# A graph kernel's first pairs: scores spread on chip, roots per graph, constants moved behind the first propagation

## The chip, the cores and the metric

The kernel runs on one core of a Trainium2 chip. The metric is the device time of one execution in microseconds (us); several executions are made and their median is given. All engines of the core run side by side, each taking its own instructions in the order in which they were written: TensorE (PE; its weight loads are PEld), VectorE (DVE), ScalarE (ACT), GpSimd (POOL), and SyncE (SP), which here only issues DMAs. ACT issues some DMAs too.

## The reference

There are 128 graphs of 128 nodes with 512 features (x) and a 0/1 adjacency matrix each (adj). Two layers are applied, each followed by a residual and a normalization over the features. Layer 0 is graph attention with 8 heads of 64 units, layer 1 a hypergraph convolution used twice.

```
# layer 0
feats   = einsum('bnf,hfu->bhnu', X, W)
dense   = e_self[..., :, None] + e_neigh[..., None, :]     # feats . a_self, feats . a_neigh
dense   = leaky_relu(dense, 0.2) + NEG_BIG * (1 - A)
out     = relu(softmax(dense) @ feats + b)                 # heads side by side: 512 features
x       = layernorm(x + out)
# layer 1
conv(x, W) = Dn * (H @ (Be * (H^T @ (x @ W^T)))) + b       # H = (adj != 0)
h       = layer_norm(relu(conv(x, W1) + b1), gamma, beta)  # 1024 features
x       = layernorm(x + conv(h, W2) + x)
```

Everything is float32.

## The kernel before, in words

The work is cut into 64 pairs of graphs. Nothing is a loop at run time: a Python list `todo` of (due time, function, arguments) is sorted by due time and walked once, and each function writes its instructions to the engines. Only the order counts; the due times are sort keys (period T = 38.6), not times on the chip. Steps of a pair are spread over about five periods (`lag`), so that several pairs are in work at once. A dictionary `first` overrides the key of single steps of the first pairs, and a second list places steps that only pairs 0 and 1 have.

For one pair, the stages are as follows.

- Loads: x, adjacency (a), its first row spread over the partitions (w), and block-wise copies (xb, ab) for pairs from 2 on, whose transposes are made by DVE (L385, L421). Pairs 0 and 1 have their transposes made by PE (L397, L410).
- Nodes and edges: `nodes` (L360 to L369) and `edges` (L423 to L428) make the two degree factors, `scale_edges` (L435) scales, `propagator` forms the product pd on PE, and `r_evict` (L451) makes R from it and from the node factors dnb, which go through DRAM to be spread.
- Features: x times the attention weights w0 (pf). Each head has two extra weight columns, so that the self and neighbour scores come out beside the features. Pairs from 2 on use a seven-product scheme on sums of blocks; pairs 0 and 1 use plain products (L523) and copies (L533).
- Scores: the neighbour scores are transposed by DVE (`rows`, L542), written to DRAM (rd, L550 or L552) and read back spread over all partitions (nb, L570). POOL adds the mask (L589), ACT applies the leaky step with the self score as bias (L605), DVE takes the largest (nm, L611), ACT the exponential (L619), each for a quarter (graph g, half q of the heads) at a time.
- Attention: the exponentials are transposed (eT; for pair 0 by PE, L651, and copied, L652), multiplied with the features and a column of ones (pav, L677 or L703), divided (rden, y; L713, L714), joined with x (L751), and normalized: moments (L759, L760), ve (L765), the root on POOL (rs, L767), and the normalization on ACT (L785 to L794).
- Propagation and layer 1: pz = y times R on PE, copied to zT by ACT (`z_evict`, L829), block differences zS on POOL (L840), the hidden layer in seven products phX, phY, phW, which DVE sums (h, L866) and ACT finishes (relu L881, square L892), its squares summed by POOL (L904), then the output layer (py), the second propagation (pq), and the last normalization and store.

The prologue also makes constants. The score columns of w0 are made by products of the raw weights with the attention vectors, DVE doing the self and POOL the neighbour vector (`prepare_first`, L234, L238), from vectors that two DMAs spread over the partitions. Seven-product sums of w0 (`prepare_first_sums`, L226), of w1 (`prepare_hidden`, L249) and of w2 follow. gamma and beta are folded into w2: column sums of w2 on PE (pv, L276, `prepare_output`), spread by two products gw and bw (L288), and each block of w2 scaled and shifted by DVE (L300, 16 instructions).

[...] PE's pieces of 64 columns (`columns`, L97) are written in pairs to two halves of a bank.

Of the kernel before, what the change touches and what calls it, by code (L numbers as in the profile page):

```python
# [8 lines left out]
F32 = mybir.dt.float32  # L9
AF = mybir.ActivationFunctionType  # L10
# [3 lines left out]
EPS = 1e-5  # L14
# [6 lines left out]
def kernel(  # L21
# [143 lines left out]
    def everywhere(t, ap, queue):  # L165
        queue.dma_start(t, ap.partition_broadcast(P))

    as_bc, an_bc = (
        work.tile([P, F], F32, tag="eb", name=n, bufs=2) for n in ("as_bc", "an_bc")
    )  # L170
# [6 lines left out]
    everywhere(an_bc, a_neigh, nc.scalar)  # L177
    everywhere(as_bc, a_self, nc.scalar)
# [6 lines left out]
    vec_rows = work.tile([3 * KH, P], F32, tag="neg", name="vec_rows", bufs=2)  # L185
    for i, ap in enumerate((gamma, beta, b1)):
        nc.sync.dma_start(vec_rows[i * KH:(i + 1) * KH], ap.rearrange("(k p) -> k p", p=P))
# [20 lines left out]
    nc.gpsimd.memset(mhalf, -0.5)  # L208

    fts = []  # L210
# [16 lines left out]

    def prepare_first(half):
        for n, (dst, raw, j) in list(enumerate(w0_blocks))[2 * half:2 * half + 2]:
            nc.scalar.copy(dst[:, :, :, 2:], raw)  # L230
            for c, bc in enumerate((as_bc, an_bc)):
                t = work.tile([P, KF // 2, HH, U], F32, tag=(("o", "xS"), ("o", "zS"))[n % 2][c],
                              name=f"wa{n}{c}", bufs=(2, 1)[c])
                (nc.vector, nc.gpsimd)[c].tensor_tensor(  # L234
                    t, raw, bc[:, j * QU:(j + 1) * QU].rearrange("p (h u) -> p h u", h=HH)
                    [:, None].to_broadcast([P, KF // 2, HH, U]), op=ALU.mult,
                )
                nc.vector.tensor_reduce(dst[:, :, :, c], t, AX.X, ALU.add)  # L238

    def prepare_first_sums():  # L240
        second_sums(nc.vector, [w0_sb[:, i] for i in range(7)], w0_12)
# [9 lines left out]
    gbs = const.tile([P, KH, 2], F32, name="gbs")  # L251
    made = {}
# [12 lines left out]
    def prepare_rows():  # L265

        made["sel"] = work.tile([2, 2, P], F32, tag="zT", name="sel")
        nc.gpsimd.tensor_copy(
            made["sel"], ident[:2, :2].unsqueeze(2).to_broadcast([2, 2, P])
        )  # L270

    def prepare_output():
        pv = made["pv"] = [bank(f"pv{j}") for j in range(2)]
        for blk, i, j in w2_blocks:
            for k in range(KH // 2):
                nc.tensor.matmul(  # L276
                    pv[j][:2, :QU], gbs[:, i * KH // 2 + k, :], blk[:, k, :],
                    start=(i == 0 and k == 0), stop=(i == 1 and k == KH // 2 - 1),
                )

    def prepare_output_sums():
        made["sums"] = const.tile([2, F], F32, name="sums")
        for j in range(2):
            nc.vector.tensor_copy(made["sums"][:, j * QU:(j + 1) * QU], made["pv"][j][:2, :QU])
# [108 lines left out]
    def x_transpose_first(p, s):  # L393
        s["px"] = [bank(f"px_{p}_{g}") for g in range(2)]
        for g in range(2):
            for k in range(KF):
                nc.tensor.transpose(  # L397
                    s["px"][g][:, k * N:(k + 1) * N],
                    s["x"][:, g].rearrange("p (f k) -> p k f", k=KF)[:, k], ident,
                )  # L400

    def x_transpose_out(p, s, g):
        if g == 0:
            s["xT"] = work.tile([P, 2, KF, N], F32, tag="xT", name=f"xT_{p}")
        nc.scalar.copy(s["xT"][:, g].rearrange("p k n -> p (k n)"), s["px"][g])
# [110 lines left out]
    def plain_features(p, s, i):  # L516
        if i == 0:
            s["pf"] = [[bank(f"pf_{p}_{g}{j}") for j in range(2)] for g in range(2)]
        for j in range(2):
            w = (w0_sb[:, 0], w0_12, w0_sb[:, 1], w0_sb[:, 2])[2 * i + j]  # L520
            for g in range(2):
                for k in range(KF // 2):
                    nc.tensor.matmul(  # L523
                        s["pf"][g][j][:, :FW], s["xT"][:, g, i * KF // 2 + k, :],
# [4 lines left out]
    def plain_features_out(p, s):  # L529
        s["ft"] = fts[p]  # L530
        for j in range(2):
            for g in range(2):
                (nc.vector.tensor_copy if g or p else nc.scalar.copy)(  # L533
                    s["ft"][:, g, j * HH:(j + 1) * HH, :UW], by_head(s["pf"][g][j])
                )

    @step(1, 25.0)
    def spread_rows(p, s):
# [7 lines left out]
        shape = [B, NB, B] if p == 0 else [NB, B, B]  # L546
        rd = s["rd"] = dram.tile(shape, F32, tag="rd", name=f"rd_{p}")
        if p == 0:
            for b in range(NB):
                (nc.sync, nc.scalar)[b % 2].dma_start(rd[:, b, :], rows[b * B:(b + 1) * B])  # L550
        else:
            nc.sync.dma_start(rd.rearrange("b c j -> (b c) j"), rows)  # L552

    def blocked(p, t):

        dims = "p (h b j) -> p b h j" if p == 0 else "p (b h j) -> p b h j"
        return t.rearrange(dims, b=NB, h=H)

    @step(1, 27.0)
    def neighbours(p, s):  # L560
        s["nb"] = work.tile([P, 2, H * N], F32, tag="nb", name=f"nb_{p}")
        for g in range(2):
            dst, src, hs = s["nb"][:, g, :], s["rd"], slice((2 + g) * H, (3 + g) * H)
            if p == 0:
                src = src[hs].rearrange("h b j -> (h b j)")
            else:
                dst = dst.rearrange("p (b x) -> p b x", b=NB)
                src = src[:, hs, :].rearrange("b h j -> b (h j)")
            queue = nc.scalar if p == 0 and g == 1 else nc.sync
            queue.dma_start(dst, src.partition_broadcast(P))  # L570
# [10 lines left out]
    def scores(p, s, g, hs):  # L581
        return blocked(p, s["nb"][:, g, :])[:, :, hs, :]
# [10 lines left out]
    def leaky(p, s, g, q):  # L593
        if (p, g, q) == (0, 1, 1):

            hs = slice(HH, H)
            t = s["nb"][:, g, HH * N:].rearrange("p (h j) -> p h j", h=HH)
            nc.vector.tensor_tensor(
                t, t, s["ft"][:, g, hs, 0:1].to_broadcast([P, HH, N]), op=ALU.add
            )  # L600
            nc.vector.scalar_tensor_tensor(t, t, SLOPE, t, op0=ALU.mult, op1=ALU.max)
            return
# [33 lines left out]
    def e_transpose(p, s, g, q):  # L636
# [6 lines left out]
        )  # L643

    def e_transpose_first(p, s, g, q):
        if (g, q) == (0, 0):
            s["eT"] = work.tile([P, 2, H, N], F32, tag="eT", name=f"eT_{p}")
        t = bank(f"pet_{g}{q}")
        for h in range(HH):
            n = (q * HH + h) * N  # L650
            nc.tensor.transpose(t[:, h * N:(h + 1) * N], s["nb"][:, g, n:n + N], ident)  # L651
        (nc.scalar.copy if q else nc.vector.tensor_copy)(  # L652
            s["eT"][:, g, q * HH:(q + 1) * HH, :].rearrange("p h n -> p (h n)"), t
        )
# [52 lines left out]
    def attended(p, s, g):  # L707
        if g == 0:
            s["y"] = work.tile([P, 2, F], F32, tag="y", name=f"y_{p}")
        rden = small.tile([P, 2, HH], F32, tag="rden", name=f"rden_{p}_{g}")  # L710
        for q in range(2):
# [410 lines left out]
    for t, fn, *args in (  # L1122
# [14 lines left out]
    T = 38.6  # L1137
    todo = [
        (11.1, prepare_first, (0,)), (12.0, prepare_first, (1,)), (15.45, prepare_first_sums, ()),
        (12.1, load_weights, (nc.scalar, w2_blocks, w2t, DH // 2, QU)),  # L1140
        (13.05, prepare_vectors, ()),
        (14.05, load_weights, (nc.scalar, w1_blocks[:2], w1t, F // 2, HALF)),
        (12.95, load_first_row, (1,)),
        (15.46, load_weights, (nc.sync, w1_blocks[:1:-1], w1t, F // 2, HALF)),
        (16.1, everywhere, (b2_bc, b2, nc.sync)),
        (79.0, prepare_hidden, (nc.gpsimd, 0)), (79.1, prepare_hidden, (nc.gpsimd, 1)),
        (120.7, prepare_hidden, (nc.gpsimd, 2)), (110.6, prepare_hidden, (nc.vector, 3)),
        (15.5, prepare_output_vectors, ()), (16.0, prepare_output, ()),
        (78.3, prepare_rows, ()), (78.79, prepare_output_sums, ()),
        (78.99, prepare_output_spread, (0, "gw")), (98.0, prepare_output_spread, (1, "bw")),  # L1150
        (98.1, prepare_output_bias, ()), (98.2, prepare_output_blocks, (slice(0, 1),)),
        (99.75, prepare_output_blocks, (slice(1, 2),)),
        (117.8, prepare_output_blocks, (slice(2, 3),)),
        (118.1, prepare_output_blocks, (slice(3, 4),)),
# [7 lines left out]
        ("spread_rows", 0): 13.5, ("neighbours", 0): 14.0,  # L1162
        ("nodes", 0): 12.9, ("write_nodes", 0): 12.92, ("spread_nodes", 0): 15.9,
        ("edges", 0): 14.46, ("edges", 2): 119.2,
        ("x_transpose", 2, 0): 120.5, ("x_transpose", 2, 1): 121.1, ("scale_edges", 0): 14.47, ("propagator", 0): 14.55,
        ("r_evict", 0): 97.845,
        ("spread_rows", 1): 15.72, ("nodes", 1): 15.55, ("write_nodes", 1): 15.85,
        ("edges", 1): 110.4, ("scale_edges", 1): 110.5, ("neighbours", 1): 80.1,
        ("propagator", 1): 121.7, ("spread_nodes", 1): 80.3, ("r_evict", 1): 121.8,
        ("leaky", 0, 1, 1): 77.65, ("leaky", 0, 0, 1): 73.6, ("largest", 0, 0, 1): 75.3,  # L1170
# [105 lines left out]
```

## Time and profile before

| what | value |
|---|---|
| median of 3 executions | 2398.43 us (2396.28 to 2400.03) |
| the profiled execution itself | 2395.3 us |
| its span, first to last instruction | 2393.4 us |
| busy in the span | PE 2360.8, DVE 2089.6, POOL 1825.6, ACT 1528.5 |
| busy from 0 to 47.2 us (first pz) | PE 34.28, DVE 32.09, POOL 22.13, ACT 18.23 |
| busy from 47.2 to 87.06 us (second pz) | PE 37.88, DVE 39.13, POOL 34.69, ACT 24.09 |

A line of a timeline gives the start, the duration, the engine, the line of the kernel, the operation, the tile written and the tiles read, and the number of instructions merged in it (x32); in brackets stands how long the engine had been idle before it and what it waited for. The chain of waits is the list of work that ended last, followed back from the end: at each moment it names the one piece that everything later depended on. Busy time is no bound by itself: an engine that is idle nearly everywhere can still hold the one instruction that the others wait for.

### The profile page before, as it was taken

To read this page: it belongs to the slowest core of one execution; us is meant where nothing else is said; L and a number is where in the kernel's file an instruction comes from. 1 tells how busy PE (TensorE), PEld (TensorE's weight loads), DVE (VectorE), ACT (ScalarE), POOL (GpSimd) and SP (SyncE) were. 2 spreads that over 40 slices of the span, in tenths; PEclk is the share of its full clock that TensorE was granted. 3 is DMA by queue.
4 is the path that set the end of the run, shared out by engine and by line. 5 is a ranking of instruction groups with operands and counts; after the bars stand their busy time and mean duration, and the time that the engine had idled before them with its cause. 6 is when DMAs were issued, how large, how long until landed. Compare 5 with 4: busy or idle time off the path is not lost.

```text
span 2393.4 us, 80729 instructions
## 1 busy us (share of the span) xinstructions
PE 2360.8 (99%) x32309; PEld 2026.8 (85%) x32309; DVE 2089.6 (87%) x4456; ACT 1528.5 (64%) x4481; POOL 1825.6 (76%) x2060
## 2 busy tenths in 40 slices
PE   7899999999999999999999999999999999999998
PEld 6788887888888888888888888888888888888886
DVE  7989888898898898898898888988988988988975
ACT  4565765756667667667667666666676676676662
POOL 5877786777877877877877778778778778778774
PEclk9999999999999999999999999999999999999999
DMA  6555454555554555555545555544545555555541
GB/s 197 133 148 150 143 144 134 159 143 147 151 148 144 149 148 148 151 143 154 144 142 157 141 147 155 146 146 147 150 143 153 147 150 139 148 156 140 149 128 37
DMA packets 431134, 347.09 MB, mean 145 GB/s; under 512 B 151440, under 2 KB 380328, under 8 KB 430760
## 3 DMA queue, kind: packets, MB, share of 16 engines
q1 hardware_dynamic: 427288, 337.46, 49.5%
q8 instruction: 256, 4.19, 0.7%
q10 hardware_dynamic: 3472, 4.47, 0.6%
q14 instruction: 118, 0.97, 0.2%
HBM read 239.08 MB, written 102.73 MB: 143 GB/s over the span
## 4 chain that ended last, share of the span: by engine, by line
PE 89%; DMA 4%; DVE 3%; ACT 1%; POOL 1%; issue 1%; SPq 1%; DVEq 0%; POOLq 0%; ACTq 0%
PE phX L97 17%; PE pyX L97 17%; PE pfX L97 8%; PE pyW L97 8%; PE phW L97 8%; PE pav L703 5%; PE phY L97 4%; PE pz L97 4%; PE pfW L97 4%; PE pq L97 4%; PE pyY L97 4%; PE pfY L97 2%; DMA ed<-nb 1%; PE pd L97 1%; DMA nb<-rd 1%
## 5 line engine op out<-in xcount | busy, mean ns | idle before, releaser
L344 ACT COPY py<-pyX 128x257 f32<-128x257 f32 x189 | 70.7, 374 | 538.5 <-PE pyX L97 465.6
L97 PEld LDWEIGHTS phX<-zS,w_sb 128*64 128x64 f32 x6144 | 350.6, 137 | 36.3 <-POOL ft L742 23.1
L97 PE MATMUL phX<-zS,w_sb 128*64 128x128 f32 x6144 | 373.4, 273 | 2.6 <-ACT ph L344 2.6
L904 POOL TENSOR_TENSOR sq<-sq 128x512 f32<-128x512 f32 (+2 forms) x384 | 343.9, 896 | 20.1
L589 POOL TENSOR_TENSOR nb<-nb,neg 128x512 f32<-128x512 f32 x256 | 319.9, 1284 | 23.1 <-DMA nb<-rd 12.7
L605 ACT ACTIVATE nb<-nb,ft 128x128 f32<-128x128 f32 x1020 | 325.1, 392 | 13.7 <-POOL nb L589 13.7
L619 ACT ACTIVATE nb<-nb,nm 128x128 f32<-128x128 f32 x1024 | 319.4, 392 | 4.2 <-DVE nm L611 4.0
L767 POOL TENSOR_TENSOR rso<-veo,mhalf 128x2 f32<-128x2 f32 x63 | 44.2, 701 | 338.4 <-DVE veo L765 338.4
L97 PE MATMUL pyX<-w_sb,hS 128*64 128x257 f32 x2016 | 245.1, 380 | 0.0
L97 PE MATMUL pyX<-w_sb,h 128*64 128x257 f32 x2016 | 243.7, 379 | 0.5 <-ACT py L344 0.5
L97 PE MATMUL pyW<-w_sb,hS 128*64 128x256 f32 x2016 | 243.3, 378 | 0.0
L881 ACT ACTIVATE h<-h,vecs 128x128 f32<-128x128 f32 x768 | 239.4, 394 | 2.0 <-DVE h L866 1.4
L611 DVE TENSOR_REDUCE nm<-nb 128x4 f32<-128x512 f32 x256 | 175.2, 684 | 48.8 <-ACT nb L605 46.2
L97 PEld LDWEIGHTS pyX<-w_sb,h 128*64 128x64 f32 x2016 | 173.7, 136 | 46.2 <-ACT py L344 0.9
L97 PEld LDWEIGHTS pyW<-w_sb,hS 128*64 128x64 f32 x2016 | 174.7, 136 | 43.6 <-issue 0.3
L742 POOL TENSOR_TENSOR ft<-ft,b_bc 128x512 f32<-128x512 f32 x128 | 203.9, 1613 | 6.1 <-ACT ft L533 6.1
L97 PEld LDWEIGHTS pyX<-w_sb,hS 128*64 128x64 f32 x2016 | 168.7, 137 | 38.7 <-issue 0.8
L640 DVE STREAM_TRANSPOSE eT<-eb 128x512 f32<-128x512 f32 x252 | 163.5, 685 | 5.7 <-DMA eb<-ed 4.7
L805 DVE SCALAR_TENSOR_TENSOR o<-y,b_bc 128x512 f32<-128x512 f32 x128 | 164.7, 1325 | 0.0
L1006 DVE SCALAR_TENSOR_TENSOR y<-y,rsh,bw_bc 128x512 f32<-128x512 f32 x126 | 150.1, 1229 | 14.9 <-POOL rsh L1002 14.9
L469 POOL TENSOR_TENSOR hS<-h 128x512 f32<-128x512 f32 x126 | 162.1, 1287 | 0.0
L892 ACT ACTIVATE sq<-h 128x512 f32<-128x512 f32 x256 | 160.6, 629 | 2.1
(178 smaller groups left out, 5672.4 us busy)
## 6 DMA issues: line engine op xcount, KB each, us to landing
nb<-rd SPq DMA_DIRECT2D x127, 512.0 KB, 5.6
ed<-nb SPq DMA_DIRECT2D x126, 512.0 KB, 3.4
eb<-ed SPq DMA_DIRECT2D x504, 128.0 KB, 2.9
x<-in_x_dram SPq DMA_DIRECT2D x64, 512.0 KB, 4.0
out_dram<-o SPq DMA_DIRECT2D x63, 512.0 KB, 2.9
xb<-in_x_dram SPq DMA_DIRECT2D x248, 128.0 KB, 5.5
a<-in_adj_dram SPq DMA_DIRECT2D x64, 128.0 KB, 2.4
w<-in_adj_dram SPq DMA_DIRECT2D x128, 64.0 KB, 5.0
```

The lines of the kernel that those rows point to most:

```text
L97: nc.tensor.matmul(to[rows], lhs[:, rows], rhs, start=start, stop=stop, skip_group_check=True)
L469: engine.tensor_tensor(t[:, i], in0, in1, op=op)
L589: nc.gpsimd.tensor_tensor(t, t, neg[:, :, None, :].to_broadcast([P, NB, HH, B]), op=ALU.add)
L605: nc.scalar.activation(t, t, AF.Prelu, bias=s["ft"][:, g, h, 0:1], alpha=SLOPE)
L611: nc.vector.tensor_reduce(s["nm"][:, g, hs], scores(p, s, g, hs).rearrange("p b h j -> p h b j"), AX.XY, ALU.max, negate=True,)
L619: nc.scalar.activation(t, t, AF.Exp, bias=s["nm"][:, g, h:h + 1])
L640: nc.vector.transpose(s["eT"][:, g, hs, :].rearrange("p h (b i) -> p h b i", b=NB), s["eb", g][:, :, hs, :].rearrange("p b h j -> p h b j"),)
L742: nc.gpsimd.tensor_tensor(t, t, b0_bc.rearrange("p (h u) -> p h u", h=H), op=ALU.add)
L805: nc.vector.scalar_tensor_tensor(s["o"][:, g, :], s["y"][:, g, :], 2.0, b2_bc, op0=ALU.mult, op1=ALU.add)
L881: nc.scalar.activation(dst[:, k, :], src[:, k, :], AF.Relu, bias=b1_sb[:, c:c + 1])
L892: nc.scalar.activation(s["sq"][:, g, q * KH // 2:(q + 1) * KH // 2, :], hid(s, g, q), AF.Square, scale=DH ** -0.5,)
L904: nc.gpsimd.tensor_tensor(t[:, :n, :], t[:, :n, :], t[:, n:2 * n, :], op=ALU.add)
```

## The change

All of it is in the prologue and in the first pairs; from pair 2 on the steps and their keys are unchanged.

- The two attention vectors are loaded as single rows on ACT's queue and spread by two products with a row of ones (`prepare_scores`); the vector for POOL is copied out of PSUM by ACT. gamma, beta and b1 (`vec_rows`) move from SP's queue to ACT's.
- The scores of pair 0 no longer go through DRAM. DVE copies the neighbour columns into `spread`, PE transposes it, and four sets of products with `heads` (a spread identity, 32 rows per quarter) put each score row on all partitions in PSUM. DVE, not POOL, adds the mask (`first_masked`), and each quarter has its own leaky, largest, exponential and transpose step. All leaky steps of pair 0 are now ACT's.
- The attention of pair 0 is divided and its root taken for each graph by itself (`first_root`), and DVE, not ACT, normalizes (`first_normalize`).
- The features of pair 1 are computed graph by graph between pair 0's steps, and its scores written and read back graph by graph (`second_rows`, `second_neighbours`).
- The sums of w0 move from DVE to POOL. The w1 loads all go on SP's queue. pair 1's first rows, nodes and edges, the vectors' transpose and copies (`prepare_vectors`, `prepare_output_vectors`), the column sums of w2 and all of its scaling come later than before. pv now uses 32-column products on four strips of one bank, and the sums are copied by ACT in one piece.
- The w1 sums (`prepare_hidden` 0 and 1) keep their keys 79.0 and 79.1; pair 0's last root has the key 75.2, its propagation 115.8.

```diff
-    everywhere(an_bc, a_neigh, nc.scalar)
-    everywhere(as_bc, a_self, nc.scalar)
+    a_rows = work.tile([1, 2, F], F32, tag="eb", name="a_rows", bufs=2)
+    for c, ap in enumerate((a_self, a_neigh)):
+        nc.scalar.dma_start(a_rows[:, c], ap[None, :])
...
+    nc.vector.tensor_reduce(one, ident.rearrange("p (c r) -> p r c", c=NB), AX.X, ALU.add)
+    heads = work.tile([P, HH, P], F32, tag="chain_2", name="heads")
+    for t in (heads, made["sel"]):
+        nc.gpsimd.tensor_copy(
+            t, one[:, :t.shape[1]].unsqueeze(2).to_broadcast(list(t.shape))
+        )
...
+    def prepare_scores():
+        for c in range(2):
+            t = made["a", c] = bank(f"a_bc{c}")
+            nc.tensor.matmul(t, ones, a_rows[:, c], start=True, stop=True)
+        t = work.tile([P, F], F32, tag="eb", name="an_bc", bufs=2)
+        nc.scalar.copy(t, made["a", 1])
...
-        second_sums(nc.vector, [w0_sb[:, i] for i in range(7)], w0_12)
+        second_sums(nc.gpsimd, [w0_sb[:, i] for i in range(7)], w0_12)
...
+    def prepare_output():
+        t = made["pv"] = bank("pv")
+        for n in range(2):
+            for j in range(2):
+                for c in range(NB):
+                    k = 2 * c + n
+                    blk = w2_blocks[2 * (k // (KH // 2)) + j][0]
+                    nc.tensor.matmul(
+                        t[c * B:(c + 1) * B, j * QU:(j + 1) * QU], gbs[:, k, :],
+                        blk[:, k % (KH // 2), :], start=(n == 0 and j == 0), stop=(n == 1),
+                        skip_group_check=True,
+                    )
...
+    def score_spread(p, s, g, q):
+        t = s["pn", g, q] = bank(f"pn_{g}{q}")
+        rows = slice((2 * g + q) * B, (2 * g + q + 1) * B)
+        for h in range(HH):
+            nc.tensor.matmul(
+                t[:, h * N:(h + 1) * N], heads[rows, h, :], s["rows"][rows, :], start=True,
+                stop=True,
+            )
+
+    def first_masked(p, s, g, q):
...
+        nc.vector.tensor_tensor(
+            s["eb", g][:, q * HH:(q + 1) * HH, :],
+            s["pn", g, q].rearrange("p (h j) -> p h j", h=HH),
+            s["neg"][:, g, None, :].to_broadcast([P, HH, N]), op=ALU.add,
+        )
...
+    def first_root(p, s, g):
...
+        nc.vector.tensor_scalar(ve, s["mv", "a"][:, g, 1:], EPS, None, op0=ALU.add)
+        nc.gpsimd.tensor_tensor(s["rs", "a"][:, g:g + 1], ve, mhalf[:, :1], op=ALU.pow)
```

The keys that set the order around the first propagation, of the changed kernel (unchanged: `prepare_hidden`, `masked`, `leaky` of pair 1):

```
(79.0, prepare_hidden, (nc.gpsimd, 0)), (79.1, prepare_hidden, (nc.gpsimd, 1)),
(117.0, prepare_output, ()), (117.05, prepare_output_sums, ()),
(119.7, prepare_output_spread, (0, "gw")), (121.65, prepare_output_spread, (1, "bw")),
...
(73.45, prepare_vectors, ()), (73.6, prepare_output_vectors, ()),
(0, 72.7, attended, 1, (0,)), (1, 72.9, plain_features, 0, (1,)),
(0, 73.4, attended, 1, (1,)), (1, 73.5, plain_features, 1, (1,)),
("residual", 0, 1): 74.2,
(0, 75.2, first_root, 1), (0, 75.9, first_normalize, 1),
("leaky", 1, 0, 0): 113.0, ("masked", 1, 0, 0): 98.0,
```

## The prediction

> **What bounds the kernel now.** I read the page's totals and slices first, then the timeline of PE, the chain of waits, and the timeline of the other engines over the first 60 us.
>
> ```profile
> span 2393.4 us, 80729 instructions
> PE 2360.8 (99%) x32309; PEld 2026.8 (85%) x32309; DVE 2089.6 (87%) x4456; ACT 1528.5 (64%) x4481; POOL 1825.6 (76%) x2060
> PE   7899999999999999999999999999999999999998
> ```
>
> PE is full except in the first slice. So the body is PE's work, and the change, which is all in the first pairs, can move the time only by moving the moment at which PE reaches its steady pace. The propagation of each pair (pz) is the mark. From PE's timeline:
>
> ```profile
> 47.23 3.68 PE L97 MATMUL pz<-R,y 128*64 128x128 f32 x32 [4.05 <-ACT y L794]
> ...
> 87.06 1.94 PE L97 MATMUL pz<-R,y 128*64 128x128 f32 x32
> ...
> 128.79 1.94 PE L97 MATMUL pz<-R,y 128*64 128x128 f32 x32
> ...
> 166.00 1.95 PE L97 MATMUL pz<-R,y 128*64 128x128 f32 x32
> ...
> 202.37 1.94 PE L97 MATMUL pz<-R,y 128*64 128x128 f32 x32
> ```
>
> The steady period is 36.37 (166.00 to 202.37). The first three are 39.83, 41.73 and 37.21: 9.66 over. The first pz also waits 4.05 and takes 3.68 where later ones take 1.94. Who makes the long periods is in the chain of waits:
>
> ```profile
> 44.99 0.17 DVE vea L765
> 45.16 0.34 DVE R L451
> ...
> 50.51 1.13 DVE w_sb L249
> ...
> 52.97 2.40 DVE w_sb L300 x6
> 55.37 0.60 DVE nm L611
> ...
> 58.88 2.10 DVE xT L385 x2
> 60.97 0.57 DVE h L866
> 61.54 0.33 DVE R L451
> 61.88 0.60 DVE nm L611
> ```
>
> From 39 to 62 the chain is DVE's, and it comes back to DVE from 74.7 to 97. In the first period DVE is busy 39.1 of 39.9. So what counts is when DVE has done its list, up to the sums h (L866, the second ends at 63.07), not when PE starts pz. Last, POOL and ACT around pz, from the timeline of all engines:
>
> ```profile
> 35.71 2.37 POOL L249 TENSOR_TENSOR w_sb<-w,w_sb 128x1024 f32<-128x1024 f32 x1 [2.50 <-DMA w<-in_w1t_dram]
> ...
> 38.16 2.38 POOL L249 TENSOR_TENSOR w_sb<-w_sb 128x1024 f32<-128x1024 f32 x1
> ...
> 45.24 0.72 POOL L767 TENSOR_TENSOR rsa<-vea,mhalf 128x2 f32<-128x2 f32 x1 [4.70 <-DVE vea L765]
> ```
>
> The two sums of w1 (4.83) lie ahead of the root, in time in which POOL has nothing else; it then waits 4.70 for DVE.
>
> [...] idle 4.05, then 3.68 against 1.94. [...] the 32 records of pz take 1.75, 0.055 each, where a record of 264 columns at full width takes 0.233. [...] here rows, DRAM and nb cost 7.2 (20.72 to 27.94).
>
> **The change, part by part** (times from the span's start, in the order in which the changed program puts instructions on each engine).
>
> *Attention vectors by products.* Two broadcasts (256 KB each) go, five small loads on ACT's queue come. ACT issues 5 instead of 2 (0.47 each) ahead of its 1.28 table load: free at 4.4. [...] Two products of 512 columns: 1.12 each in the row gw at full clock, twice that cold: 2.9 to 7.3. ACT's copy of the second (0.59): 7.9. Fewer bytes let x land 1.4 earlier (0.5 MB at 370 GB/s), which gains nothing: DVE and POOL bind. DVE makes the first of twelve column steps at 5.1 and then stands: POOL has the new spreads (heads 0.7, sel 0.39, zeros 0.31, from the row sel and the memset row), which wait for DVE's `one` at 6.9. POOL's first product of raw weights ends at 9.6. DVE's remaining ten steps at 0.72 (twelve took 7.09 to 15.73) end at 16.8, before 15.73: 1.1 lost. The four last feature products (0.466 each) end at 18.75; before 20.16, because pair 1's transposes no longer stand between.
>
> *Scores on chip.* The DRAM way goes (7.2). On DVE stand nodes (1.35, 16.9 to 18.25) and, after pt, edges and their scaling (2.13 as from 20.88): 21.25. Four column copies at 0.19 (row rden): 22.0. Transpose and copy, 0.5: 22.5. Each bank of spread scores is four products of 128 columns, 0.9 at pf's rate; I take 0.9, it could be 0.45. The masks (DVE, PSUM in, 0.7 as the row eT) follow from 23.4: first one done 24.2, POOL's before 29.2. It is 5.0 ahead there.
>
> *Softmax by quarters.* ACT: four instructions take 1.28. Leaky (0,0) and (0,1) 24.25 to 26.8, exponentials to 29.4, leaky of graph 1 to 31.9. PE: pair 1's features fill, four products (1.87) from 26.1 and again from 28.25 to 30.1, so pet (0,1) is at 30.65 to 31.15 though its input is ready at 29.4. DVE: eT (0,1) to 31.9, y, largest (1,0) to 33.2 (leaky was done at 30.65), y, residual and moments (1.63), largest (1,1) to 36.1. ACT: exponentials 33.2 to 34.5 and 36.1 to 37.4, pair 1's copies 0.76, eT (1,1) to 38.8. PE: pav (1,1) to 39.4. DVE: both halves of y to 40.1.
> *A wait.* On DVE, gbs (2 x 0.17) now stands before the residual of graph 1 and waits for vecs, whose transpose stands on PE behind four feature products (39.4 to 41.25). So gbs ends 42.05: 1.6 lost. Residual, moments, ve: 43.85. The root per graph on POOL, 0.72: **44.6**. Before: 45.96. The normalization on DVE (0.75) ends 45.4. R needs dnb, issued by SP at about 20: covered.
>
> *pz.* PE works through pair 1's products up to 43.6, so pz is warm: 43.6 and 45.4 to 46.3, before 50.7. **4.4 ahead.**
>
> *What lies behind the root.* Prices as above. POOL's FIFO now has both w1 sums behind the second root: 44.6 to 49.4; then pair 1's mask (1.28) to 50.7. On ACT the leaky step (1,0,0) stands ahead of z_evict and waits for that mask: 52.0. So zT ends 52.6, before 49.84. PE has pv left (16 products, four at a time: 1.75, bounds 1.75 and 7.0), ends 48.05 and idles 4.5, so phX is likely cold (+1.75; bounds 0 and 2). phX and phY end 57.9, gw 1.12: 59.0, then bw 1.12, both formerly in PE's idle time. DVE: rows, nodes and edges of pair 1 (3.7) now come after 45.4 and end near 49.1; a late w (issued behind nb, some 5 us) would delay them to 50.7, still hidden. hidden3 to 50.7. largest (1,0,0) waits for leaky: to 52.6. largest (1,0,1) waits for zT, sums, zT, leaky: to 55.7. hT of pair 2 to 57.9. Then all 16 scalings of w2, of which before 8 lay ahead of pz and the rest at 52.2 to 55.3: they wait for gw, 12 from 59.0 to 63.7, largest 64.3, 4 to 65.9, xT 67.9, h 68.5, R, largest 69.5, h **70.1**. Before 63.07: **7.0 late**.
>
> Both engines' sums agree: DVE has 19.5 from 45.4 to the end of that list, before 18.1 from 45.0, and 5.1 of waits (0.3, 1.3, 2.4, 1.1). Cheap edits: w0's sums go to POOL (4 x 1.3, 24.2 to 29.5, nothing waits); bias stays hidden; SP's w1 loads wait for dnb and have 17 us to spare; xb and b2 come at 42 to 45, used past 58; nb by graph is issued near 41 and 48.5, so the third mask may start at 53, covered by phY.
>
> From there on the order is that of before, and the chain stays with relu, then DVE to 97, so the delay is carried. I take off 0.5 for DVE instructions that overlap (four scalings per 1.56, not 4 x 0.475, and the like). **+6.5.** The profiled execution is 2395.3, 1.9 over its span; it becomes 2401.8. The median of the runs is 3.1 above that execution: 2404.9, so 2405.
>
> **Rivals.**
> 1. *The later periods swallow it.* For: 9.66 of excess. Against: DVE makes this excess too. With half swallowed, some +2: 2400.5. Chance 0.25.
> 2. *Faster: the front packs tightly.* Columns at DVE's pace from 4.3 (12.9), features 14.8, first mask 20.3, then ACT's 10.2 without gaps, the tail 4.1, the root: 36.2 instead of 44.6. Each us there is a us of the result; it decides below 37.6. It gives -2 with POOL's order as it is, -6 if DVE need not wait besides: 2392.5. Against: the fixed orders above. Chance 0.07.
> 3. *Slower still.* POOL works beside DVE in the front, and one column product took 1.50 instead of 0.72, deg 1.24 for 0.17: +11, 2409.5. Chance 0.12.
>
> **How the numbers follow.** The forecast, 2405, gets 0.56, with its own range 2401 to 2409 from the bounds of pn, pv, the cold clock and the landing times (about 3 each way in all). A measurement tells about 0.2% (4.8) from no change. Below 2393.6: rival 2, 0.07. Within: rival 1 and the low end of the forecast, 0.31. Slower: 0.62. Eight in ten: 2396 to 2411.
>
> **What would show it.** The second root ends near 44.6; pz warm by 46.3; an idle gap of PE after pv until POOL's mask and ACT's leaky are done near 52; the scalings after gw near 59; the second h near 70; the second pz near 93.5. It is wrong if the root is at 38, if zT doesn't wait for the leaky step, or if the pz of pair 3 is not some 6 us later than 166.00.

## The result, and the profile after

| | before | changed |
|---|---|---|
| median of five executions | 2398.43 us | **2433.88 us** (2431.97 to 2442.2) |
| ratio | | 1.0153, 95% interval 1.0134 to 1.0172 |
| profiled execution, span | 2395.3, 2393.4 | 2442.2, 2440.4 |

The change makes the kernel slower by 35.5 us. I had forecast 6.5 and a range up to 2411: the sign was right, the size was not. The profiled execution is the slowest of the five, 8.3 us above their median; no trace shows which part of it the other four do not have.

The page of the changed kernel, its span, its engines, the instruction queues, and the shares of the chain of waits:

```profile
span 2440.4 us, 80804 instructions
PE 2380.4 (98%) x32346; PEld 2005.8 (82%) x32346; DVE 2084.1 (85%) x4457; ACT 1527.3 (63%) x4486; POOL 1823.0 (75%) x2065
...
q8 instruction: 256, 4.19, 0.7%
...
PE 50%; DMA 24%; DVE 7%; POOL 7%; ACT 5%; SPq 4%; issue 2%; DVEq 0%; POOLq 0%
```

The chain of the kernel before, from its page:

```profile
PE 89%; DMA 4%; DVE 3%; ACT 1%; POOL 1%; issue 1%; SPq 1%; DVEq 0%; POOLq 0%; ACTq 0%
```

PE looks as full as before, but it holds 50% of the chain where it held 89%, and DMA 24% where it held 4%. The marks, from PE's timeline of the changed kernel (pairs 1 to 4):

```profile
102.42 1.83 PE L97 MATMUL pz<-R,y 128*64 128x128 f32 x30
...
143.14 1.94 PE L97 MATMUL pz<-R,y 128*64 128x128 f32 x32
...
180.63 1.95 PE L97 MATMUL pz<-R,y 128*64 128x128 f32 x32
...
217.24 1.95 PE L97 MATMUL pz<-R,y 128*64 128x128 f32 x32
```

Against 87.06, 128.79, 166.00 and 202.37 they are 15.4, 14.4, 14.6 and 14.9 late; this lateness is called the shift from here on. That is the first loss, made before 102 us. The second comes later, where the steps have the order of before: in the profiled execution the shift grows to 47.0 at pair 52 and then stands still. Of pairs 3 to 61 the periods exceed 36.37 by 38.4 us in sum (before: 6.1, of which 5.4 in pairs 5 to 9).

**The first loss.** The timelines of the changed kernel around the first propagation; first SP, whose lines are DMA issues:

```profile
50.70 0.34 SPq L623 DMA_DIRECT2D rd<-rows  x1
56.00 0.34 SPq L392 DMA_DIRECT2D dd_d<-dr  x1
56.44 0.39 SPq L628 DMA_DIRECT2D nb<-rd  x1
...
58.88 3.92 SPq L137 DMA_DIRECT2D ab<-in_adj_dram  x4
```

DVE in the same time:

```profile
47.98 2.55 DVE L837 TENSOR_SCALAR y<-y,mva,rsa 128x512 f32<-128x512 f32 x1 [0.68 <-POOL rsa L611]
...
66.06 0.45 DVE L436 STREAM_TRANSPOSE hT<-ab 128x256 f32<-128x256 f32 x1 [6.45 <-DMA ab<-in_adj_dram]
...
67.37 1.65 DVE L318 SCALAR_TENSOR_TENSOR w_sb<-w_sb,vecs,gw 128x256 f32<-128x256 f32 x4
...
77.75 0.68 DVE L933 TENSOR_TENSOR h<-ph,phW 128x512 f32<-128x512 f32 x1
```

POOL, at the third mask of pair 1:

```profile
62.53 1.26 POOL L676 TENSOR_TENSOR nb<-nb,neg 128x512 f32<-128x512 f32 x1 [7.23 <-DMA nb<-rd]
```

And PE, at the third product of the hidden layer:

```profile
65.81 3.68 PE L97 MATMUL phX<-zS,w_sb 128*64 128x128 f32 x32 [5.20 <-POOL zS L907]
```

SP writes dd only when DVE has made dr (55.76), and the load of nb of graph 1 and the four loads of ab stand behind that write. So POOL's third mask, and zS behind it, and PE behind that, wait for nb; and DVE waits 6.45 for ab, with the sixteen scalings of w2 queued behind. gw, for which I had made the scalings wait, was there at 60.6. The second h ends at 78.4 instead of 63.1. The chain of waits of the changed kernel runs through the same links:

```profile
50.67 3.51 DVE w L378 x4
54.20 1.14 DVE dn L383
...
55.76 0.22 DVE dr L387
56.00 0.34 SPq L392
...
56.44 6.03 DMA nb<-rd
62.48 3.45 DMA ab<-in_adj_dram
...
66.06 0.46 DVE hT L436
```

Its first two lines, DVE's nodes of pair 1, are slow as well. The first of these instructions, in the changed kernel and in the kernel before:

```profile
50.60 2.28 DVE L378 SCALAR_TENSOR_TENSOR w<-a,w 128x128 f32<-128x128 f32 x1
```

```profile
25.66 0.29 DVE L360 SCALAR_TENSOR_TENSOR w<-a,w 128x128 f32<-128x128 f32 x1
```

From there to the end of dr it takes 5.4 us, before 1.4; POOL works beside it nearly all that time, on the w1 sums and the masks (47.90 to 55.31). One load of pair 2 has moved too, though the list of the change says that its keys are as before: its blocks of x (xb) have the key 76.1 instead of 16.2, and SP issues them at 43.60 instead of 33.44.

**The second loss.** One event goes with the long periods: how long SP waits between the write of the score rows (rd) and the load of nb. SP's queue in a normal period of the kernel before:

```profile
961.08 0.34 SPq L552 DMA_DIRECT2D rd<-rows  x1
962.51 1.39 SPq L570 DMA_DIRECT2D nb<-rd  x2
```

and in a long period of the changed kernel:

```profile
950.48 0.34 SPq L643 DMA_DIRECT2D rd<-rows  x1
953.61 0.94 SPq L653 DMA_DIRECT2D nb<-rd  x2
```

From the issue of the write of 16 KB to that of nb it takes 1.43 here and 3.13 there. Over all kernels of this study it is near 1.45 (quick) or between 2.2 and 3.7, in the middle 2.9 (slow), with 14 of 826 in between. From nb on everything on SP follows later, up to ed, eb and eT of the next period, for which PE then waits: in the whole span 24 times, 24.1 us, against twice, 4.0 us, before. From the lists of waits (total, times, longest), the changed kernel first:

```profile
PE pav L770 <- DVE eT L718: 24.1, 24, 1.9
```

```profile
PE pav L703 <- DVE eT L640: 4.0, 2, 2.3
```

In the DMA traffic from 25.0 to 26.4 us after pz, in the same two periods, one packet stands out. The kernel before:

```profile
DMA packets 717, 0.09 MB, mean 61 GB/s; under 512 B 717, under 2 KB 717, under 8 KB 717
```

The changed kernel, with its line of the queue q8 (packets, MB, share of 16 engines):

```profile
DMA packets 707, 0.10 MB, mean 72 GB/s; under 512 B 706, under 2 KB 706, under 8 KB 706
...
q8 instruction: 1, 0.02, 6.0%
```

The packet on q8 has 16 KB and takes 6.0% of 16 engines' 1.40 us, which is 1.34 us of one DMA engine. The page calls the kind of q8 "instruction", and I take its packets to carry PE's own instructions, since the counts agree. q8 moves 4.19 MB in 256 packets. PE's records (the instructions as the trace counts them) are 32346 products and as many weight loads, and with 912 semaphore instructions that is 65604: 256.3 to a packet, 63.9 bytes each. In the kernel before the same count is 65534, again on 256 packets: 256.0. What such a packet costs is what the experiments put to the test.

### The profile page after: what moved, and what is told of

Same layout as the page of the kernel before. It is cut to its first block, busy times and chain, and to the rows that moved or that the text cites. A ratio compares the mean times of both kernels' runs of the same rounds, so it can differ in the third digit from the quotient of the medians.

```text
span 2440.4 us, 80804 instructions
## 1 busy us (share of the span) xinstructions
PE 2380.4 (98%) x32346; PEld 2005.8 (82%) x32346; DVE 2084.1 (85%) x4457; ACT 1527.3 (63%) x4486; POOL 1823.0 (75%) x2065
## 3 DMA queue, kind: packets, MB, share of 16 engines
q8 instruction: 256, 4.19, 0.7%
## 4 chain that ended last, share of the span: by engine, by line
PE 50%; DMA 24%; DVE 7%; POOL 7%; ACT 5%; SPq 4%; issue 2%; DVEq 0%; POOLq 0%
DMA ed<-nb 11%; PE pyX L97 10%; PE phX L97 9%; DMA nb<-rd 6%; PE pyW L97 5%; PE pfX L97 4%; PE phW L97 4%; DMA eb<-ed 4%; DMA rd<-rows 3%; SPq L709 3%; PE pav L770 3%; PE pz L97 3%; POOL nb L676 3%; PE phY L97 3%; PE pyY L97 3%; ACT nb L683 2%
## 5 line engine op out<-in xcount | busy, mean ns | idle before, releaser
L362 ACT COPY py<-pyX 128x257 f32<-128x257 f32 x189 | 70.6, 374 | 567.6 <-PE pyX L97 491.8
L676 POOL TENSOR_TENSOR nb<-nb,neg 128x512 f32<-128x512 f32 x252 | 314.5, 1281 | 72.4 <-DMA nb<-rd 54.5
L697 ACT ACTIVATE nb<-nb,nm 128x128 f32<-128x128 f32 x1008 | 314.5, 391 | 5.5 <-DVE nm L689 5.5
L97 PEld LDWEIGHTS pyX<-w_sb,h 128*64 128x64 f32 x2016 | 167.5, 136 | 52.4 <-ACT py L362 0.9
L770 PEld LDWEIGHTS pav<-ft,eT 128*64 128x64 f32 x3968 | 132.7, 138 | 37.6 <-POOL hS L484 18.4
```

Of the source, the lines that this page charges most:

```text
L97: nc.tensor.matmul(to[rows], lhs[:, rows], rhs, start=start, stop=stop, skip_group_check=True)
L676: nc.gpsimd.tensor_tensor(t, t, neg[:, :, None, :].to_broadcast([P, NB, HH, B]), op=ALU.add)
L697: nc.scalar.activation(t, t, AF.Exp, bias=s["nm"][:, g, h:h + 1])
L770: nc.tensor.matmul(t[rows], s["eT"][:, g, h, rows], s["ft"][:, g, h, 2:], start=True, stop=True,)
```

## The experiments

**Three orders in the prologue.** From the changed kernel: e1 makes the w1 sums early, e2 puts nb of graph 1 ahead of the write of dd, e4 has both and an early vecs.

```diff
-(79.0, prepare_hidden, (nc.gpsimd, 0)), (79.1, prepare_hidden, (nc.gpsimd, 1)),     # e1, e4
+(69.0, prepare_hidden, (nc.gpsimd, 0)), (69.1, prepare_hidden, (nc.gpsimd, 1)),
-("nodes", 1): 76.5, ("write_nodes", 1): 76.55,                                       # e2, e4
+("nodes", 1): 77.1, ("write_nodes", 1): 77.15,
-(73.45, prepare_vectors, ())                                                         # e4
+(53.05, prepare_vectors, ())
```

> The two w1 sums on POOL get the keys 69.0 and 69.1 instead of 79.0 and 79.1, so that they stand ahead of pair 0's roots, where POOL is idle from about 29 to 38 us. If DVE's normalization of graph 1 took 2.55 us because POOL's sum of w1 ran beside it, it now takes 0.6 to 0.8, and the first three masks of pair 1 come about 4.8 us earlier, from 47.9; the third still waits for nb of graph 1, so the third pz moves by 2 us only (from 143.1 to about 141). Rival: the 2.55 us is DVE's own, and the line stays at 2.5. The total falls by the 2 us or, if the later long periods depend on how the prologue ends, by up to 20.

> nodes and write_nodes of pair 1 get the keys 77.1 and 77.15, behind the load of nb of graph 1 (77.0) on SP. If that load was late because SP's queue stood behind the write of dd, which waits for DVE, nb of graph 1 is issued near 52.3 instead of 56.4, POOL's wait of 7.23 for it shrinks to about 3, and PE's wait of 5.20 for zS to about 1. Gain at the third pz 1 to 4 us. Rival: the wait is the load's own time (rd written, then 6 us for 512 KB beside the xb loads), then POOL's and PE's waits stay within 1 us and nothing is gained.

> Both moves above, and the transpose of the vectors at 53.05 instead of 73.45, so that gbs need not wait for it. If these three are what my sum missed in the prologue, the wait of 2.88 for vecs goes, the second root ends near 45, pz of graph 1 near 49, and the third pz comes near 136 (before 128.8, changed kernel 143.1, my sum 135.3). Rival: other waits move into their place, and the third pz stays above 140. What the later periods then do is open: if the long periods of 36.6 to 38.8 depend on the state that the prologue leaves behind, their sum changes too; if they belong to the program, it stays at 18 to 32.

Measured: 2435.89, 2435.62 and 2436.11 us, all 1.015 times before, like the change itself (each with an interval of 0.0015 to 0.002 to either side, some 4 to 5 us). In e1 the normalization of graph 1 takes 0.55, from DVE's timeline:

```profile
47.70 0.55 DVE L837 TENSOR_SCALAR y<-y,mva,rsa 128x512 f32<-128x512 f32 x1 [0.68 <-POOL rsa L611]
```

so POOL's sum beside it had made it 2.55. The masks come 3.9 earlier (48.78), dr ends at 52.35 instead of 55.97, and at pair 4 the shift is 11.8 instead of 14.9. In e2 nb of graph 1 goes out at 52.90 and PE waits 2.03 for zS instead of 5.20; the third pz gains 1.0, the low end of what I expected. In e4 the wait for vecs is gone and the second root ends at 45.05, close to my 44.6. But the third pz is at 139.4, 142.1 and 142.2 (143.1): the rival of e4 is right, other waits are in their place. PE's for zS is back at 5.19, since the write of rd takes SP from 48.01 to 52.37, and DVE's for ab has grown to 8.65 (e4, DVE's timeline):

```profile
63.93 0.45 DVE L436 STREAM_TRANSPOSE hT<-ab 128x256 f32<-128x256 f32 x1 [8.65 <-DMA ab<-in_adj_dram]
```

**A pause of PE.** My first theory of the second loss was a chain of transfers that is late once and feeds itself.

```diff
+    def dummy():
+        t = bank("dummy")
+        for i in range(8):
+            nc.tensor.matmul(t, ident, b0_bc, start=(i == 0), stop=(i == 7))
+    todo.append((7 * T - 0.05, dummy, ()))
```

> The changed kernel with eight products of 128x512 (identity times the spread bias, results unused) put on PE ahead of pair 4's propagation, some 8 to 9 us of PE. Theory A: the long periods come from a chain of transfers that trails PE and feeds itself (late nb, late sums, late blocks of x, late ed and eb, late eT, late rows, late nb), and a pause of PE lets it catch up: the periods after pair 6 are 36.4, and the total is 2398 + 15 + 9 = about 2422, below the changed kernel's 2434. Rival: the long periods belong to the program or to chance, and the total is 2434 + 9 = 2443.

Measured: 2455.76. Both were wrong. The pause took 7.13, the next period was 36.42, and then the long periods came back and, unlike in the changed kernel, went on to the last pair: 49.4 us in sum. The first theory fell here. What had changed for good was only PE's list, longer by 16 records.

**Shifting the fetch.** Small products whose results nobody reads, put into PE's list, shift where the 16 KB packets fall in a period; besides, they cost PE their own time, once, ahead of the loop.

```diff
+    def fill(n):
+        t = bank("fill")
+        for i in range(n):
+            nc.tensor.matmul(t[:, :1], ident[:1], ident[:1, :1], start=True, stop=True)
+    todo.append((5.0, fill, (37,)))        # f3, from before; (110,) in f4
+    todo.append((121.35, fill, (75,)))     # f1, from the changed kernel; (24,) in f2
```

> The kernel before, with 37 one-column products of one row put on PE ahead of everything, where PE is idle up to 8.08 us. Nothing else changes. Theory F: PE's own instructions come by DMA in pieces of 16 KB (queue q8, 4 in a period); the piece that is fetched at about 25.8 us of a period keeps one DMA engine busy just when the score rows (rd) are written, so that nb starts 1.5 us later and the chain of transfers behind it trails; the place of the fetch moves by one PE record per period, so the kernel before left it at pair 16 and the changed kernel, with 37 records more, at pair 53. Then this kernel too has long periods up to about pair 53, and its total is about 2400 + 15 to 25 = 2415 to 2425. Rival (the state that the prologue leaves behind, or the order and places of the changed program): PE's list changes in nothing that matters, and the total stays within 3 us of 2400.

> The same with 110 such products, so that the fetch of pair p comes where the kernel before has it at pair p - 110 + 128 = p + 18, past the bad place from the start. Theory F: no long periods from pair 5 to 16, which cost 6 us in the kernel before, and a total of about 2394; the last periods lie where no run has been, and could lose again. Rival: 2400, or worse by what 110 products cost.

> The changed kernel with 75 such products ahead of PE's third product of the hidden layer of pair 0, where PE waits some 5 us for zS in any case. The fetch of pair p comes where the kernel before has it at pair p - 37 - 75 + 128 = p + 16. Theory F: no long periods after pair 5, the shift of 14 to 15 us at pair 4 is all that is left, and the total is 2412 to 2416. Rival: 2434 or more.

> The same with 24 products: the fetch comes where the kernel before has it at pair p - 61, in the bad place from the first pair to the last (as with the pause of eight products, 16 records, p - 53). Theory F: long periods to the end, total 2434 to 2445. Rival (any fill of PE's idle time there helps[...]): below 2425, as with 75.

Measured: f3 2418.01, f4 2441.62, f1 2456.08, f2 2418.87. Only f3 hit its number, and that by luck: 9.5 of its 22 us are the shift that the products themselves make by pair 4, and its long periods run from pair 15 to the end, not up to 53. f2 came out where its rival had it, below 2425. That any fill of PE's idle time helps is not shown by it: at pair 4 it is only 3.2 us ahead of the changed kernel, the rest is gained in later periods, in which the clock granted to PE is 1.00 of full speed in the changed kernel as well (from 217 to 2400); and f1, for which the rival said the same, got slower (32.7 us late at pair 4). Two of my assumptions were wrong. Such a product is two records, not one (the page of f2 has 32394, 48 more than 32346), and a record takes 0.15 to 0.21 us, where the records of pz take 0.055: in f4 the products occupy PE from 1.79 to 48.9, and the second pz is 40 us late. With the records counted right, all kernels up to here fall on one line. Let r be the records added over the kernel before. Then rd is slow in pair p when (p - r) modulo 128 lies outside 16 to 67. 128 records with their weight loads are 256 instructions, by the count above one packet. A pair has 504 products, as many weight loads and 14 semaphore instructions in PE's trace, 1022 in all, which by that count is two less than four packets hold; so from pair to pair the packet's place moves by one record, and 37 records more move it by 37 pairs. The ends 16 and 67 are read off these kernels, so they are a fit; of the next kernels g2 and g3 test it at a new r.

**The test of both theories.** g1 repairs SP's order and puts POOL's third mask of pair 1 behind the first two zS. g2 adds e1, the early vecs and 76 records; g3 is the kernel before with 114 records. g4 takes the blocks ab out of the way of rd.

```diff
-p * T + (28.5 if p == 2 else 20.5), load_edges                                        # g1, g2
+76.15 if p == 2 else p * T + 20.5, load_edges
-("masked", 1, 1, 0): 98.2,                                                            # g1, g2, with e2's lines
+("masked", 1, 1, 0): 119.85,
+            nc.tensor.matmul(t[rows, :B], ident[:, rows], ident[:, :B], start=True, stop=True)   # fill of g2, g3
+    todo.append((119.72, fill, (38,)))                                                # g2
+    todo.append((3 * T - 0.02, fill, (57,)))                                          # g3
-p * T + (28.5 if p == 2 else 20.5), load_edges                                        # g4
+p * T + (28.5 if p == 2 else 28.4), load_edges
```

> The changed kernel with three moves in the order: nodes and write_nodes of pair 1 behind nb of graph 1 (as in e2), the blocks of the adjacency of pair 2 (ab) at 76.15 instead of 105.7, so that SP issues them near 46 instead of behind all that waits for pair 1's nodes, and POOL's third mask of pair 1 behind the first two differences zS. Theory: the prologue's loss is SP's queue, in which the loads of nb and ab stand behind a write that waits for DVE. Then DVE's wait of 6.45 for ab and PE's of 5.20 for zS go, the second h comes near 70 instead of 77.75, and the shift of the pz of pair 4 against the kernel before falls from 14.9 to 7 to 9. PE's list has as many records as in the changed kernel, so the later long periods stay, and the total falls by the same 6 to 8, to about 2427. Rival: another wait takes their place and the shift stays above 12.

> g1, with the w1 sums and the vectors' transpose early (as in e4), and with 38 small products (64 columns of weights, 32 moving; two records each, 76 in all) on PE behind gw, which put the instruction fetch of pair p where the kernel before has it at pair p + 15. Theory F: long periods only in the last dozen pairs; the shift at pair 4 is 5 to 7, and the total is 2398 + 6 - 6 + 4 = 2402 (2398 to 2407). Rival: the fetches' place is not what counts, and the later periods cost some 20 more.

> The kernel before with 57 such small products (114 records, 4 us) ahead of pair 0's propagation, where PE waits 4.05 us for y. The fetch of pair p comes where the kernel before has it at pair p + 14. Theory F: the long periods of pairs 5 to 10, 6 us, go, some 3 to 4 us come in the last dozen pairs, and the total is 2395 to 2397, a little under the kernel before. Rival: no gain, 2398 to 2400.

> The changed kernel with the blocks of the adjacency (ab) of pairs from 3 on loaded behind nb and dnb (key 28.4 instead of 20.5), so that no queue of small packets stands ahead of the score rows (rd) when the instruction fetch comes. Theory F, with the fetch acting through what is queued on its DMA engine: rd lands in 1.5 us again, the long periods go or shrink, and the total is 2405 to 2420. Rival: the fetch delays rd by itself, or ab is late for DVE, and the total stays at 2434 or rises.

Measured: g1 2423.26 (1.0124, 1.0110 to 1.0139), g2 2398.87 (1.0015, 1.0008 to 1.0023), g3 **2391.73** (0.9981, 0.9975 to 0.9988), g4 2461.85. g1 gains a little more than I expected, g2 lies within its range. g3 is below its own, but so is the kernel before beside it, 2395.99 where I had assumed 2398 to 2400.

In g1 DVE's wait for ab is gone, and the second h ends at 70.6, where my sum had 70.1 (DVE's timeline):

```profile
58.19 0.43 DVE L436 STREAM_TRANSPOSE hT<-ab 128x256 f32<-128x256 f32 x1
...
69.89 0.69 DVE L933 TENSOR_TENSOR h<-ph,phW 128x512 f32<-128x512 f32 x1
```

PE's wait for zS is 1.71 instead of 5.20:

```profile
60.88 1.97 PE L97 MATMUL phX<-zS,w_sb 128*64 128x128 f32 x32 [1.71 <-POOL zS L907]
```

The shift at pair 4 falls from 14.87 to 6.66. g2 and g3 gain in the later periods: at pair 4 g2 stands at 6.62, with the normalization and the nodes free of POOL's sums, and it is 24.4 us faster than g1. g3 keeps the pz of pair 4 within 0.7 of before and gains 4.3 us against the kernel before beside it (2395.99): pairs 5 to 7 now have 36.37, and pair 8 has 37.23 instead of 40.42. It is the fastest kernel of the study, and has nothing of the change in it.

The fit against the profiled kernels, pairs 3 to 61 ("slow": over 2.2 us from rd to nb):

| kernel | r | slow pairs by the fit | rd slow among them | rd slow elsewhere | periods over 36.37, us |
|---|---|---|---|---|---|
| before | 0 | 3 to 15 | 9 of 13 | 3 of 46 | 6.1 |
| changed | 37 | 3 to 52 | 44 of 50 | 0 of 9 | 38.4 |
| e5 | 53 | all | 56 of 59 | | 49.4 |
| f3 | 74 | 14 to 61 | 47 of 48 | 0 of 11 | 19.7 |
| f2 | 85 | 25 to 61 | 35 of 37 | 1 of 22 | 19.1 |
| f1 | 187 | all | 58 of 59 | | 34.9 |
| f4 | 220 | 32 to 61 | 28 of 30 | 2 of 29 | 13.6 |
| g1 | 37 | 3 to 52 | 43 of 50 | 0 of 9 | 23.3 |
| g2 | 113 | 53 to 61 | 7 of 9 | 3 of 50 | 3.0 |
| g3 | 114 | 54 to 61 | 4 of 8 | 4 of 51 | 3.5 |
| g4 | 37 | 3 to 52 | 43 of 50 | 0 of 9 | 62.1 |

e1, e2 and e4, with the r of the changed kernel, are slow in 43, 44 and 47 of the same 50 pairs and in 1, 0 and 0 of the other 9.

The single packets in the traces show the same without a fit. Of the 826 writes of rd in pairs 3 to 61 of all 14 kernels, 469 have a packet of q8 that starts between 0.2 us before SP's issue and 1.1 us after it, and 468 of these are slow; of the other 357, 54 are. All 14 slow writes outside the fit's pairs meet an 8 KB packet of the other instruction queue, q14, that starts 0.8 to 1.2 us after the issue. By its bytes q8 holds PE's whole list, so those packets are not PE's: what delays the write is the packet, not a PE that runs out of instructions. And the period that follows a slow write is 0.62 us over 36.37 on average (473 writes, g4 left out), the one that follows a quick write 0.04 (281).

g4 missed, and both halves of its rival are right: DVE waits for the late ab 45 times, 142.9 us from 255 to 1965, and rd is as slow as ever. But it shows the mechanism best, since nothing else is queued. SP's queue in a slow pair of g4:

```profile
954.04 0.33 SPq L643 DMA_DIRECT2D rd<-rows  x1
956.80 0.92 SPq L653 DMA_DIRECT2D nb<-rd  x2
```

The DMA traffic of g4 from 953.30 to 954.70:

```profile
DMA packets 1, 0.02 MB, mean 12 GB/s; under 512 B 0, under 2 KB 0, under 8 KB 0
...
q8 instruction: 1, 0.02, 4.7%
```

And from 954.70 to 956.90, in 40 slices of 0.055 (share of the engines in tenths, and rate):

```profile
DMA  0004751000000000011000000000000000000000
GB/s 0 0 0 72 105 82 21 0 0 0 0 0 0 0 0 0 7 7 5 0 0 0 0 0 0 0 0 0 0 0 0 0 0 0 0 0 0 0 0 0
DMA packets 144, 0.02 MB, mean 7 GB/s; under 512 B 144, under 2 KB 144, under 8 KB 144
```

The fetch starts at 954.56 and holds one engine for 1.05 us (4.7% of 16 engines' 1.40), to 955.61. Of the 144 packets of rd 135 go in a burst from 954.87 to 955.09; the other nine, a sixteenth of them, follow from 955.61 to 955.77, at a rate of 7 GB/s, when the fetch has ended. That these nine had to wait for the engine of the fetch is my inference from their number and their time, since the views do not name a packet's engine. SP issues nb only after these last few, at 956.80.

## Why the prediction was wrong

**Steps that held.** The front up to 42 us: the first mask at 23.06 (forecast 23.4), the columns done at 15.4 (16.8). Later gw, done at 60.6 (59.0), and pv four at a time: in g2 its 32 records, 32 wide and 256 columns long, take 1.94 (49.15 to 51.09), as long as the 8 records of pf, 128 wide and 264 columns long, just before. In the changed kernel, whose granted clock is 0.62 from 52.2 to 55.0, they take 2.95 (52.21 to 55.16). The rival that the later periods swallow the delay is refuted, since the shift is 14.4 to 15.4 at pairs 1 to 4.

**Terms of the sum that were mis-sized.** The wait of gbs for vecs is 2.88 and not 1.6, and the second root ends at 47.94 and not at 44.6. The normalization is 2.55 and not 0.75, since POOL's w1 sums run beside it; e1 shows this. Rows, nodes and edges of pair 1 on DVE take 6.8 (50.45 to 57.28) and not 3.7. e1 and e4 take away part of this and gain at most 3.7 at a mark and nothing in the total that the runs can tell. With SP's order repaired nothing of it is left to see (a shift of 6.66 in g1, where it is all there, and of 6.62 in g2, where it is taken away). Too large was the landing of the attention rows, 2.9, an estimate of mine with no number of the trace behind it: ACT issues these rows at 0.72 and PE starts on them at 2.33, so the trace has 1.6. The +1.75 that I gave phX behind an idle PE fell on another product: phX waited 0.68 and took 1.97, and the third product of the hidden layer waited 5.20 and took 3.68, with the granted clock at 0.50 from 65.8 to 69.4. In the kernel before it is 0.50 from 47.2 to 51.0, in the pz of 3.68 that waited 4.05.

**The step that failed in the prologue** is a sentence among the "cheap edits": nb by graph "is issued near 41 and 48.5, so the third mask may start at 53, covered by phY", and with it "hT of pair 2 to 57.9". I had moved nodes and their write, and not counted what stands behind that write on SP: nb at 56.44 and ab at 58.88, landed at 62.5 and 66.1. So the second h ended at 78.4 and not at 70.1. g1 takes these waits away, the h ends at 70.6, and the shift of 6.66 that stays agrees with my 6.5. Its cause, the scalings of w2 behind pz, was not tried by itself, so the agreement may hold some luck. The load had been in front of me: between the lines that I showed of the chain before, from 45.51 to 50.24, the list names SP and the load of ab, and not DVE:

```profile
45.51 0.36 SPq L576
...
45.92 0.50 SPq L137
...
46.47 3.78 DMA ab<-in_adj_dram
```

DVE is busy all that time and reads ab at 55.88, so ab had some 5.6 us to spare. The change issues it 13 us later.

**The step that failed behind it** is "From there on the order is that of before", so that "the delay is carried". The order is that of before, but the list is 37 records longer, and that moves PE's instruction fetches against the score rows by 37 pairs: the kernel before leaves the slow place at pair 16, the changed one at pair 53. I had looked at which work is done, not at where in the list it lies. In medians, each against the kernel before beside it, the changed kernel is 35.5 over, g1 27.3 and g2 2.9. So 8.2 are SP's order (with POOL's mask, which g1 moves too), 24.4 the fetches (g2's other edits gain nothing by pair 4), and the 2.9 left are about my 6.5, less the 6.1 that the kernel before itself loses to the fetches, plus the 3.0 that g2 still loses. No rival of mine had this. Rival 3 has the sign of the miss, and its cause, POOL beside DVE, is a part of the first loss: e1 takes some of it away and is 3.1 us better at pair 4, but it is not the part that lasts behind the prologue.

**What stays open.** Why the same slow rd costs 0 in one period and over 2 us in the next; the periods often alternate. No kernel kept rd off the engine of the fetch, so its cost is shown by moving the fetches alone. Why the profiled execution of the changed kernel loses some 8 us more than the others. And why SP goes on 1.0 us after the last packet of rd in g4, where in the kernel before it needs about 0.4.

## What to carry to other kernels

When a step is moved past others on a queue, list what stands behind its waits on that queue, loads for later pairs too. Where a long unrolled kernel changes speed in periods whose order did not change, compare the landing of its smallest dependent transfer and look at the instruction queue: if the small write coincides with a 16 KB fetch, a few dozen cheap instructions ahead of the loop can be worth more than a better order (here 24.4 us against 8.2). And a trial that adds or removes instructions ahead of a long loop changes more than it says, so compare kernels at equal counts before a few us are put down to an edit.

## What the runs showed of the hardware that was not expected

- An instruction fetch of 16 KB holds one DMA engine for some 1.05 us (g4) to 1.34 us (the changed kernel), and nb, which waits for the 16 KB of rd, is then issued 2.9 us behind it (the middle of the slow ones of all kernels here) instead of 1.45. An 8 KB packet of q14 does it too (2.2 to 2.7 us). The periods of e5 lose 49 us of 2456 in this way.
- A product of one row and one column of float32 counts as two records and takes 0.15 to 0.21 us for each (220 records in 47.09 us in f4, 48 in 7.17 in f2); with 64 columns of weights and 32 moving, 76 records take 2.41 us (g2).
- DVE's normalization of 128x512 takes 0.55 alone (e1) and 2.55 while POOL adds two 128x1024 tiles (the changed kernel).
